# Two more token sets routed inside the attentions, and another order of dense chunks and quads in the last mixture

## The chip, the cores and the metric

The kernel runs on one core of one Trainium2 chip. The metric is the device time of one execution in microseconds. The engines are TensorE (PE, with its weight loads shown as PEld), VectorE (DVE), ScalarE (ACT), GpSimd (POOL) and SyncE (SP). Each engine works through its own instructions; transfers run on 16 DMA engines and are started by SyncE, ScalarE or GpSimd.

## The reference

The reference is a two-layer decoder over 32 sequences of 128 tokens, so 4096 tokens of 128 features. Each layer adds a self attention, a cross attention to a context and a mixture of experts. The change concerns the second layer: the end of its attentions, and its mixture.

```python
def _L1_ffn_ref(hidden_states, gate_w, expert_bias, w1, w2, w3, sw1, sw2, sw3):
    E, TOP_K = 16, 4
    router_logits = x @ gate_w.T
    biased = router_logits + expert_bias
    _, sel = lax.top_k(biased, TOP_K)
    raw = jnp.take_along_axis(router_logits, sel, axis=-1)
    rw = jax.nn.softmax(raw.astype(jnp.float32), axis=-1)
    g = jnp.zeros((T, E), x.dtype).at[jnp.arange(T)[:, None], sel].add(rw)
    for e in range(E):
        routed = routed + g[:, e:e + 1] * _swiglu(x, w1[e], w2[e], w3[e])
    shared = _swiglu(x, sw1, sw2, sw3)
    return shared + routed
...
x = x + _L1_attn_ref(_layernorm(x, axis=-1), ...)
x = x + _L1_xattn_ref(_layernorm(x, axis=-1), ctx_1024, ctx_1024, ...)
x = x + _L1_ffn_ref(_layernorm(x, axis=-1), ...)
```

## The kernel before

**Tokens.** The 4096 tokens are eight groups of 512 (`NG`), each of four batches of 128. Two groups make a set, so there are four sets, 0 to 3, of eight batches (`NBR`). In the second mixture set 1 (groups 2 and 3, the dense pair) is computed densely: every one of its tokens goes through all 16 experts, weighted with a share that is zero for the experts not chosen. Sets 0, 2 and 3 (`SETS`) are computed by rows: a token's row is written to the place of each of its four experts, the experts run over these rows alone, and the results are read back and added.

**The second layer's attentions** (`second_layers`) are written as a list of stages. A tuple (stage, at, every, n) says that the stage's k-th piece is issued in step at + every * k. `steps` goes through the steps and issues the pieces; stages in `between` are split into small parts, and one part is put after each part of the main stages, so that VectorE's and GpSimd's small work lies between the larger pieces. From step 8 on the order within each engine is that in which the code is written. Self attention runs ahead, cross attention (`xweights`, `xaverage`, `xfinish`) follows; it takes four batches per group, one batch per step, and ends in step 45. Before each product of a batch GpSimd copies v (line 1075). Inside these steps set 0 is already prepared for the mixture: `rnorm`, `rscaled` and `rturn` of groups 0 and 1 (steps 18 to 24), `routing` (step 25), the choice in parts (`choose`), `placed` (step 33, which counts and gives each token its places) and `way_out` (from step 35: GpSimd issues 32 indirect DMAs, line 2096, four per step, each of 128 rows of 512 bytes). The normed rows of a group are kept in `xn`, the transposed ones in `hs`.

**The last mixture** (`last_layer`) is a second such list, wholly in written order, SyncE's DMAs included. Its pieces are these.

- A *quad* is four tiles of 128 rows, each of one expert; there are 12 per set, 36 in all. `rows_of` loads 256 KB of rows and four blocks of 192 KB of weights, with room for three quads at once. `rows_turned` transposes the rows (line 2176), `rows_up` makes the gate and up products and the activation (lines 2188 and 2189), `rows_down` the down product one step later, and it stores 256 KB of results.
- A *chunk* is one expert over 512 tokens. `chunk_up` issues pg and pu on TensorE, the activation on ScalarE (line 2226), the product with pu on VectorE (line 2227) and, for an expert, the product with the share (line 2229). `chunk_down` issues y. The dense pair has 2 * 17 chunks, where the 17th is the shared expert. The groups of the row sets have just the shared expert, so six more chunks, called `alone`. After its last chunk a group's x is added by TensorE, copied and stored.
- `at` says which chunks are issued in which step. `ups` and `downs` go by it. With two chunks in a step, `downs` holds chunks back, so that the y of one comes after the pg and pu of later ones; with fewer than two it issues everything that waits, in that step:

```python
        def downs(s):
            while waiting and (len(at.get(s, ())) < 2 or not at.get(s + 1)):
                chunk_down(*waiting.pop(0))
                yield
```

- `fetched` loads the shares of four experts for a group, 1 MB, broadcast from DRAM, where `send` has put them.
- `way_back` issues four gathers of GpSimd (line 2204) for a batch, and `added` adds their rows to x on VectorE (line 2215). Three batches' gathered rows have room.
- `norm`, `scaled`, `turn`, `routing`, `chosen`, `placed`, `owned` and `way_out` prepare set 1 (up to `send`) and sets 2 and 3.

Before, the first quads begin with step 0, the dense pair is prepared in steps 0 to 4, set 2 in steps 1 to 10 and set 3 in steps 5 to 20. Chunks begin in step 6, with one beside each quad up to step 23 and one beside every second quad from then on; nine dense chunks and the six alone follow from step 38 on, two per step at first, with the gathers of set 3 one batch per step.

## Time and profile before

| | |
|---|---|
| time before, three runs | 1402.74, 1413.80 and 1420.57 us; median 1413.8 |
| the profiled execution's own time | 1410.02 us |
| its span in the profile | 1408.2 us |
| mean granted TensorE clock | 0.947 |
| busy: TensorE, VectorE, ScalarE, GpSimd | 1259.3, 858.3, 577.2, 534.6 us |
| moved by DMA | 129.06 MB, 92 GB/s in the mean |
| last projection of the cross attention starts | 1119.74 us |
| first and last transposes or products of the quads | 1121.3 and 1352.1 us |
| rows scattered by GpSimd in the last 300 us (line 2096) | 64 and 12 DMAs, 0.98 us each |
| rows gathered by GpSimd (line 2204) | 96 DMAs, 0.97 us each |

Times in views of the profile are in microseconds from the span's start. A line of a timeline names start, duration, engine, source line and operation, then output<-inputs by the program's names, the shapes and how many instructions are put together; what stands in brackets is the idle time ahead of them and what ended it. PE's records of one product come in pairs, so x2 is one product of 512 columns. The line of many matrix products is that of a helper, 977, so they are told apart by the names of their tiles.

### The profile page before, as it was taken

What the parts mean: (1) busy time and instruction counts of PE and PEld (TensorE: products, weight loads), DVE (VectorE), ACT (ScalarE), POOL (GpSimd) and SP (SyncE); (2) the same over time, 40 slices, a digit from 0 to 9 for tenths busy, and PEclk for the clock granted to TensorE, in tenths of its full rate; (3) what the DMA queues carried; (4) which work ended last, traced back from release to release, by engine and by line L of the source; (5) the groups of instructions that cost most, each with busy time, mean ns of one, the idle gap of its engine ahead of it and who ended that gap; (6) DMA issues with size and microseconds to landing.
All of it is one profiled execution on the core that took longest, in us unless ns stands there. A gap on an engine that the chain in (4) does not pass through costs nothing.

```text
span 1408.2 us, 27520 instructions
## 1 busy us (share of the span) xinstructions
PE 1259.3 (89%) x10753; PEld 846.7 (60%) x10753; DVE 858.3 (61%) x2271; ACT 577.2 (41%) x848; POOL 534.6 (38%) x729
## 2 busy tenths in 40 slices
PE   3689999999999999699999988989986688799997
PEld 2357777777777787444444445656653376577753
DVE  5646767676777575385775536666674346534563
ACT  1354445454554433133232235555543434334432
POOL 5233243435341231032000214444427605575775
PEclk8789999999999999799999999989987869999999
DMA  9501111121111111455055020000001259599943
GB/s 351 177 1 32 32 31 33 32 50 34 41 31 32 32 32 37 92 112 122 14 107 122 0 97 1 3 1 2 2 1 31 84 156 334 193 337 306 326 147 96
DMA packets 89528, 129.06 MB, mean 92 GB/s; under 512 B 9872, under 2 KB 63760, under 8 KB 87984
## 3 DMA queue, kind: packets, MB, share of 16 engines
q1 hardware_dynamic: 76624, 102.59, 26.0%
q0 software_dynamic: 6144, 12.60, 3.0%
q10 hardware_dynamic: 6624, 12.05, 2.3%
q8 instruction: 87, 1.43, 0.4%
q14 instruction: 49, 0.40, 0.1%
HBM read 99.34 MB, written 27.85 MB: 90 GB/s over the span
## 4 chain that ended last, share of the span: by engine, by line
PE 64%; DVE 15%; POOL 7%; DMA 5%; ACT 4%; issue 3%; SPq 1%; DVEq 0%; ACTq 0%; POOLq 0%
PE po L977 8%; PE pg L977 7%; PE pu L977 7%; PE y L977 6%; PE pqk L977 6%; PE scores L977 4%; PE sums L977 4%; PE xscores L977 3%; POOL rows_in L2096 3%; PE pval L977 3%; DMA factor<-factors 2%; PE pyrows L977 2%; PE proj L977 2%; PE xsums L977 2%; PE qkvr L977 2%
## 5 line engine op out<-in xcount | busy, mean ns | idle before, releaser
L1280 ACT ACTIVATE e<-scores 128x1024 f32<-128x1024 f32 x128 | 124.0, 1021 | 61.5 <-PE scores L977 61.5
L977 PE MATMUL y<-sg,wide 128*128 128x512 f32 x224 | 117.6, 613 | 7.5 <-DVE sg L2229 2.6
L977 PE MATMUL pg<-hx,wide 128*128 128x512 f32 x224 | 116.0, 599 | 0.0
L977 PE MATMUL pu<-hx,wide 128*128 128x512 f32 x224 | 115.3, 596 | 0.0
L2204 POOL DMA_INDIRECT back<-rows_out,place x96 | 93.1, 970 | 37.5 <-issue 24.6
L1295 DVE STREAM_TRANSPOSE by_token<-sums 128x512 f32<-128x512 f32 x64 | 45.6, 713 | 96.7 <-PE sums L977 96.5
L1126 POOL TENSOR_SCALAR xn<-x,mv,r 128x128 f32<-128x128 f32 x80 | 67.7, 853 | 91.7 <-PE pxn L1135 82.8
L1097 POOL TENSOR_SCALAR r<-mv 128x4 f32<-128x4 f32 x48 | 11.5, 241 | 219.4 <-DVE mv L1116 219.0
L1531 ACT ACTIVATE e<-xscores 128x1024 f32<-128x1024 f32 x64 | 62.0, 1021 | 79.9 <-PE xscores L977 79.9
L1882 ACT ACTIVATE sg<-pg 128x512 f32<-128x512 f32 x72 | 43.0, 597 | 119.4 <-PE pg L977 110.4
L977 PE MATMUL sums<-e,v 128*32 128x128 f32 x2048 | 74.8, 290 | 17.2 <-POOL v L1075 17.1
L977 PE MATMUL scores<-qb,k 32*128 32x512 f32 x512 | 79.1, 689 | 11.9 <-ACT qb L1466 4.5
L1883 DVE TENSOR_TENSOR sg<-sg,pu 128x512 f32<-128x512 f32 x72 | 49.3, 685 | 61.1 <-PE pu L977 58.1
L1097 POOL TENSOR_SCALAR r2x<-mv 128x2 f32<-128x2 f32 x16 | 3.7, 234 | 212.0 <-DVE mv L1116 212.0
L977 PEld LDWEIGHTS sums<-e,v 128*32 128x32 f32 x2048 | 55.7, 115 | 46.8 <-POOL v L1075 21.6
L2096 POOL DMA_INDIRECT rows_in<-xr,place x64 | 62.9, 983 | 34.6 <-issue 18.0
L1545 DVE COPY v<-pval 128x512 f32<-128x512 f32 x64 | 43.5, 680 | 51.1 <-PE pval L977 51.1
L1579 ACT COPY av<-po 128x512 f32<-128x512 f32 x64 | 37.5, 586 | 89.6 <-PE po L977 89.5
L977 PEld LDWEIGHTS pu<-hx,wide 128*128 128x128 f32 x224 | 42.6, 191 | 52.5 <-issue 50.1
L977 PE MATMUL po<-e,v 128*64 128x128 f32 x1024 | 65.8, 281 | 8.2 <-DVE v L1545 8.2
L977 PE MATMUL po<-av,wide 128*128 128x256 f32 x256 | 64.1, 405 | 8.1 <-DVE av L1599 8.1
L977 PEld LDWEIGHTS y<-sg,wide 128*128 128x128 f32 x224 | 35.9, 189 | 58.0 <-DVE sg L1885 36.7
(300 smaller groups left out, 2913.2 us busy)
## 6 DMA issues: line engine op xcount, KB each, us to landing
row_weights<-in_w1f_dram SPq DMA_DIRECT2D x144, 192.0 KB, 4.2
factor<-factors SPq DMA_DIRECT2D x64, 256.0 KB, 5.0
share<-combined SPq DMA_DIRECT2D x32, 512.0 KB, 11.4
rows_in<-in_few SPq DMA_DIRECT2D x36, 256.0 KB, 4.1
rows<-rows_in SPq DMA_DIRECT2D x36, 256.0 KB, 5.3
rows_out<-yrows ACTq DMA_DIRECT2D x36, 256.0 KB, 4.3
share<-combined SPq DMA_DIRECT2D x8, 1024.0 KB, 7.8
wide<-in_w1f_dram SPq DMA_DIRECT2D x1, 3272.0 KB, 10.5
```

The lines of the kernel that those rows point to most:

```text
L977: last[0] = nc.tensor.matmul(*args, **kw)
L1097: nc.gpsimd.tensor_scalar(t, src, add, None, ALU.add)
L1126: eng.tensor_scalar(n[:, b, :], x[g][:, b, :], mv[:, b, 0:1], r[:, b : b + 1], ALU.subtract, ALU.mult)
L1280: nc.scalar.activation(e[-1], ps[:, bass.ts(n, 2)].rearrange("p c i s -> p (c i) s"), AF.Exp, scale=scale)
L1295: nc.vector.transpose(tt.rearrange("p i t r -> p (i t r)"), po.rearrange("p i s -> p (i s)"))
L1531: nc.scalar.activation(e[-1], ps[:, n].rearrange("p r c s -> p (r c) s"), AF.Exp, scale=scale)
L1545: nc.vector.tensor_copy(v[:, bass.ts(n, XC), :], pv)
L1579: nc.scalar.copy(avs[w][n][:, :, bass.ts(b, S)], po)
L1882: nc.scalar.activation(sg, pg, AF.Silu)
L1883: nc.vector.tensor_tensor(sg, sg, pu, ALU.mult)
L2096: sent = nc.gpsimd.indirect_dma_start(out=rows_in[n], out_offset=bass.IndirectOffsetOnAxis(ap=self.places[n][:, k, u : u + 1], axis=0), in ...
L2204: nc.gpsimd.indirect_dma_start(out=outs[n, u][:, k], out_offset=None, in_=rows_out[n], in_offset=bass.IndirectOffsetOnAxis(ap=places[n][:, ...
```

## The change

The dense pair and set 2 are now normed, scaled, turned and routed inside `second_layers`, as set 0 was. Their turned rows go into the context's tiles that are not needed any more (`more`), and set 2's normed rows as well (`kept`). `choose(1, 3)` in steps 34 to 39 makes the dense pair's weights and `send` writes them to DRAM in step 41; set 2's logits come in step 41, and its choice is finished at the start of `last_layer`. Set 0's scatters are spread over steps 35 to 45, three per step.

In `last_layer` set 2's choice is in step 0, its places in step 1, its scatters in steps 2 to 5, eight per step; set 3 is prepared in steps 0 to 14. Dense chunks begin in step 0 (one, two and two in steps 0 to 2), the quads begin with step 3 (`Q` = 2). One chunk lies beside each quad in steps 3 to 8, one beside every third from step 9 on. The 13 dense chunks left and four of the shared-expert chunks follow from step 39 (`END`) on, one per step, the last two of these in steps 56 and 58. Set 3's gathers come in steps 40, 42 and so on to 54, and `added` three steps later.

```diff
         def turn(wk, g):
-            pool = edge if g in groups(0) else wk
-            hs[g] = pool.tile([128, GT], F32, name="hx", bufs=2 if g in groups(0) else 5)
+            pool, bufs = (edge, 2) if g in groups(0) else (wk, 5)
+            hs[g] = more[g] if g in more else pool.tile([128, GT], F32, name="hx", bufs=bufs)
             by_feature(xn.pop(g), hs[g])
...
         def kept(self, g):
-            self.xn[g] = self.spare[:, g]
-            return self.xn[g]
+            if g < 2:
+                self.xn[g] = self.spare[:, g]
+            elif g * GB // NBR in SETS:
+                self.xn[g] = cx[g - 2].rearrange("p (b f) -> p b f", f=D)
+            return self.xn.get(g)
...
-        for s in range(6, NQ + 1):
-            if s < 2 * QUADS or s % 2 == 0:
-                at[s] = [todo.pop(0)]
-        for s in range(NQ + 2, 100):
-            if not todo:
-                break
-            at[s] = [todo.pop(0) for _ in range(min(2, len(todo)))]
-        for k in range(0, 4, 2):
-            at[s + k // 2] = alone[k : k + 2]
-        at[s + 3], at[s + 5] = alone[4:5], alone[5:6]
-        LAST = s + 6
+        Q = 2
+        many = {0: 1, 1: 2, 2: 2, **{s: 1 for s in range(3, 9)}, **{s: 1 for s in range(9, NQ + Q + 1, 3)}}
+        for s, n in many.items():
+            at[s] = [todo.pop(0) for _ in range(n)]
+        END = NQ + Q + 1
+        for s, item in enumerate(todo + alone[0:4], END):
+            at[s] = [item]
+        at[s + 1], at[END + 19] = alone[4:5], alone[5:6]
+        LAST = END + 21
...
-                fetches.append(((g, j), 5 if before is None else step_of[before, NS * j + NS - 1] + 1))
+                fetches.append(((g, j), 0 if before is None else step_of[before, NS * j + NS - 1] + 1))
...
-            (each(rows_turned, quads), 1, 1, NQ),
-            (several(turn, of_set(dense_n)), 2, 1, 1),
-            once(routing, dense_n, 2),
-            (lambda _: send(wk, dense_n), 4, 1, 1),
-            (several(turn, of_set(n2)), 4, 1, 1),
-            once(routing, n2, 4),
-            once(tables.owned, n2, 8),
-            (several(turn, of_set(n3)), 10, 1, 1),
-            once(routing, n3, 10),
-            once(tables.owned, n3, 14),
+            (each(rows_turned, quads), Q + 1, 1, NQ),
+            (several(turn, of_set(n3)), 2, 1, 1),
+            once(routing, n3, 3),
+            once(tables.owned, n2, 3),
+            once(tables.owned, n3, 8),
             (ups, 0, 1, LAST),
-            (each(rows_down, quads), 2, 1, NQ),
-            (each(rows_up, quads), 1, 1, NQ),
+            (each(rows_down, quads), Q + 2, 1, NQ),
+            (each(rows_up, quads), Q + 1, 1, NQ),
             (downs, 0, 1, LAST),
...
-                once(several(norm, of_set(dense_n)), None, 0),
-                once(several(scaled, of_set(dense_n)), None, 1),
-                once(several(norm, of_set(n2)), None, 1),
-                once(several(scaled, of_set(n2)), None, 2),
-                once(chosen, dense_n, 3),
-                once(chosen, n2, 5),
-                once(several(norm, of_set(n3)), None, 5),
-                once(tables.placed, n2, 6),
-                *((each(tables.way_out, batches(n2)[i::2]), 7, 1, 4) for i in range(2)),
-                once(several(scaled, of_set(n3)), None, 8),
-                once(chosen, n3, 11),
-                once(tables.placed, n3, 12),
-                (each(tables.way_out, batches(n3)), 13, 1, NBR),
-                (each(way_back, batches(0)), 21, 1, NBR),
-                (each(added, batches(0)), 24, 1, NBR),
-                (each(way_back, batches(n2)), 29, 1, NBR),
-                (each(added, batches(n2)), 32, 1, NBR),
-                (each(way_back, batches(n3)), NQ + 3, 1, NBR),
-                (each(added, batches(n3)), NQ + 5, 1, NBR),
+                once(chosen, n2, 0),
+                once(several(norm, of_set(n3)), None, 0),
+                once(tables.placed, n2, 1),
+                (each(tables.way_out, to_send(n2, 2)), 2, 1, 4),
+                once(several(scaled, of_set(n3)), None, 1),
+                once(chosen, n3, 4),
+                once(tables.placed, n3, 5),
+                (each(tables.way_out, to_send(n3, 1)), 7, 1, NBR),
+                (each(way_back, batches(0)), 20, 1, NBR),
+                (each(added, batches(0)), 23, 1, NBR),
+                (each(way_back, batches(n2)), 28, 1, NBR),
+                (each(added, batches(n2)), 31, 1, NBR),
+                (each(way_back, batches(n3)), END + 1, 2, NBR),
+                (each(added, batches(n3)), END + 4, 2, NBR),
...
-            (first(rturn), 20, 4, R),
+            (first(rturn), 20, 4, 3 * R),
...
-            (first(routing), 25, 1, 1),
+            (first(routing), (25, 33, 41), 1, 3),
             (lambda _: tables.owned(0), 36, 1, 1),
+            (lambda _: send(early, 1), 41, 1, 1),
...
-                (first(rscaled), 19, 4, R, xturn),
-                (first(rnorm), 18, 4, R),
+                (first(rscaled), 19, 4, 3 * R, xturn),
+                (first(rnorm), 18, 4, 3 * R),
...
-                (lambda u: tables.way_out(0, u), 35, 1, NBR),
+                (lambda i: tables.way_out(0, to_send[3 * i : 3 * i + 3]), 35, 1, 11),
+                (lambda _: choose(1, 3), 34, 1, 6),
...
-        mixture1 = mixture("l1f", W1F, lambda lg, _: tables.route(lg, 0), 1, True, of_expert, tables.kept)
+        route = lambda lg, n: tables.route(lg, n) if n in SETS else route_softmax(lg, edge)
+        mixture1 = mixture("l1f", W1F, route, 1, True, of_expert, {2: cx[0], 3: cx[1], 4: cx[4], 5: cx[5]}, tables.kept)
```

## The prediction

> **What bounds the kernel now.** I read the page first (TensorE is busy 1259.3 of 1408.2 us), then the busy time in stretches, then the timelines of TensorE, VectorE and GpSimd where a stretch looked thin. Columns of the first view: bounds of the stretch, its length, busy us (and instructions) of PE, PEld, DVE, ACT and POOL, granted TensorE clock, DMA share, GB/s.
>
> ```profile
> 1080.00:1100.00 20.00, 9.35 (x85) 4.40 (x88) 5.39 (x17) 5.88 (x8) 15.84 (x21) 0.74 0.09 27
> 1120.00:1140.00 20.00, 17.15 (x89) 15.81 (x90) 9.97 (x41) 6.02 (x10) 2.92 (x6) 0.65 0.71 208
> 1140.00:1160.00 20.00, 15.65 (x88) 14.05 (x87) 5.37 (x27) 8.58 (x13) 0.00 (x0) 0.66 0.44 136
> 1200.00:1220.00 20.00, 13.74 (x87) 10.26 (x85) 9.17 (x34) 6.82 (x10) 13.93 (x14) 0.98 0.37 134
> 1240.00:1340.00 100.00, 98.23 (x630) 76.13 (x630) 47.23 (x94) 42.23 (x72) 69.56 (x73) 1.00 0.99 328
> 1360.00:1380.00 20.00, 20.00 (x54) 9.31 (x53) 12.78 (x27) 4.77 (x8) 15.43 (x16) 1.00 0.22 62
> ```
>
> The reader is to see five regimes. At 1080 to 1120 the attentions end with GpSimd full and TensorE idle. At 1120 to 1160 the mixture starts at a granted clock of 0.65 with DMA half used. At 1200 to 1220 both fall off. At 1240 to 1340 TensorE and DMA are full together, at 328 GB/s. After 1352 the dense chunks run TensorE full under the last gathers.
>
> How long one step is comes from TensorE's timeline (start, us, engine, line, output<-inputs, [idle before <-releaser]).
>
> ```profile
> 1295.10 0.60 PE L2176 MATMUL prows<-in_few,rows 128*128 128x128 f32 x4
> 1298.26 0.60 PE L2176 MATMUL prows<-in_few,rows 128*128 128x128 f32 x4
> 1298.70 1.02 PE L977 MATMUL pg<-hx,wide 128*128 128x512 f32 x2
> 1303.95 0.60 PE L2176 MATMUL prows<-in_few,rows 128*128 128x128 f32 x4
> ...
> 1368.32 1.02 PE L977 MATMUL pg<-hx,wide 128*128 128x512 f32 x2
> 1370.90 1.02 PE L977 MATMUL pg<-hx,wide 128*128 128x512 f32 x2
> ...
> 1389.95 1.02 PE L977 MATMUL pg<-hx,wide 128*128 128x512 f32 x2
> 1390.82 1.02 PE L977 MATMUL pu<-hx,wide 128*128 128x512 f32 x2
> 1392.69 1.12 PE L977 MATMUL y<-sg,wide 128*128 128x512 f32 x2 [0.85 <-DVE sg L2227]
> 1394.54 1.02 PE L977 MATMUL pg<-hx,wide 128*128 128x512 f32 x2
> ```
>
> A quad without a chunk takes 3.16 us (1295.10 to 1298.26), one with a chunk 5.69. Two chunks per step flow at 2.58 us each (1368.32 to 1370.90), since `downs` lags. A lone chunk per step (the one at 1389.95 is shared-expert work) is different: its `y` stands directly behind its own `pu`, so TensorE stops 0.85 us for VectorE's product, and with its eight additions of x it takes 4.59 us. VectorE's timeline shows what a dense chunk adds to that wait:
>
> ```profile
> 1365.16 0.69 DVE L2227 TENSOR_TENSOR sg<-sg,pu 128x512 f32<-128x512 f32 x1 [1.16 <-PE pu L977]
> 1365.88 0.69 DVE L2229 TENSOR_TENSOR sg<-sg,share 128x512 f32<-128x512 f32 x1
> ```
>
> A second product, by the share, 0.72 us later. For the attentions I took every fourth sum of the cross attention, which repeats every four steps:
>
> ```profile
> 873.75 0.72 DVE L1295 STREAM_TRANSPOSE by_token<-sums 128x512 f32<-128x512 f32 x1 [1.57 <-PE sums L977]
> 905.97 0.72 DVE L1295 STREAM_TRANSPOSE by_token<-sums 128x512 f32<-128x512 f32 x1 [1.42 <-PE sums L977]
> 942.39 0.72 DVE L1295 STREAM_TRANSPOSE by_token<-sums 128x512 f32<-128x512 f32 x1 [1.43 <-PE sums L977]
> 977.50 0.72 DVE L1295 STREAM_TRANSPOSE by_token<-sums 128x512 f32<-128x512 f32 x1 [1.42 <-PE sums L977]
> 1009.61 0.72 DVE L1295 STREAM_TRANSPOSE by_token<-sums 128x512 f32<-128x512 f32 x1 [1.43 <-PE sums L977]
> ```
>
> Cycles of 32.2, 36.4, 35.1 and 32.1 us. The second and third hold the norm, scaling and turn of groups 0 and 1; the fourth holds the routing of set 0.
>
> **The change, stage by stage.** I take three stages of the profiled execution: up to the last projection of the attentions (1119.5), from there to the end of the last `pyrows` (1352.1), and from there to the end (56.1 us to 1408.2). The run itself took 1410.0, and the median shown is 1413.8.
>
> *Attentions: +8.* Four groups more are normed, scaled and turned there. Each costs what groups 0 and 1 cost, (36.4 + 35.1)/2 - 32.2 = 3.5, so 14. Two more routings are 16 logits records each, 1.85 us at full clock (981.21), so 3.6. The softmax of the dense pair is VectorE work of the kind that made the fourth cycle no longer than the first: nothing while VectorE keeps its slack (about 15 busy of 20 us at most there), 4 us without it. `send` puts eight transposes on TensorE, about 1. Together 18.6. Against that, GpSimd issues its scatters in order with the copies of v that `sums` waits for, one per 1.27 us (1113.83, 1115.10, with v at 1116.06, and TensorE waits 3.07 us for it). Scatters go out three per step over steps 35 to 45 in place of four over 35 to 42, so about eight of 32 now stand behind the last v copy: 8 x 1.27 = 10.2 off. Bounds: +18.6 if none of that is given back, -3 if the work of groups 4 and 5 fits into the waits of 1080 to 1120 (16.4 us of TensorE waiting on GpSimd and VectorE). I take 18.6 - 10.2 = +8.
>
> *Start to last quad: 232.6 becomes 213, so -20.* What leaves it: four groups' turns and two routings, at half clock 1.8 and 3.4 us each pair (1127.64, 1129.43), and the stop at 1214 to 1221, where set 2's scatters were late for its first quad. They now start about 28 us after the stage begins and end near 70, and set 2's quads come near 100. What comes in, with 0 at the last projection: the first share is fetched into memory that the attentions free, 1 MB behind that projection, landing near 7 (its median from issue is 7.8, alone less). The first dense chunk multiplies at 8, and VectorE then works in written order through set 2's choice (4.2 plus a trip to ScalarE, 14), set 3's moments (1166.3 to 1169.6 in the trace, 3.3; 17), chunks 1 and 2 (1.4 each), the places (5.3) and the scaling (2.3): 28. Only then can TensorE turn groups 6 and 7, and chunks 3 and 4 follow: 34. Step 3, with the logits, a chunk and the first quad, ends at 43. Bounds for the step's start are 16 (everything but set 3's moments, scaling and five chunks is done before 0) and 40 (share late by 6 more).
>
> Steps 4 to 14 hold seven chunks: 5 x 5.69, then two of 5.69 and four of 3.5, and 4 for set 3's places and owners: 58, so 101. Steps 15 to 38 have one chunk in three: TensorE needs (5.69 + 3.16 + 3.5)/3 = 4.12 per quad. DMA needs 0.79 MB of weights, 0.26 read and 0.26 written per quad, and GpSimd's scatters and gathers bring 0.065 MB every 1.25 us beside them, 52 GB/s: 1.31/(0.328 - 0.052) = 4.7 us. The old kernel ran one chunk per two quads there at 4.45, with DMA at 0.96 to 1.00. I take 4.5, nearer to that measured row: 24 x 4.5 = 108, and with 4 for the last share and late loads 101 + 108 + 4 = 213. So fewer chunks beside the quads buy little: DMA takes over as the bound. Ends: the early start and TensorE's 4.12 give 25 + 58 + 99 + 4 = 186; the late start and 4.9 give 49 + 58 + 118 + 4 = 229.
>
> The Trainium skill, DMA: Bandwidth & Descriptors, section Bandwidth, puts the fabric's ceiling at 435 GB/s and a core's HBM limit at about 358. The row says 328 at share 0.99, and the row decides. By 358 a quad would need 4.3 us, as an estimate from that page, and the stage would be 5 us shorter; by 435 TensorE would bind at 4.12 and it would be 9 shorter.
>
> *After the last quad: 56 becomes 89, so +33.* 21 of 34 dense chunks go beside or ahead of the quads, so 13 and the six shared-expert chunks are left, one per step. `downs` flushes whenever a step has fewer than two. Each dense one therefore costs 2.74 (1389.95 to its `y`) + 0.72 for the second product + 0.89 = 4.35 in place of 2.58. The first is half covered by the last `pyrows` (1.7 after it): 1.7 + 12 x 4.35 + 0.9 for group 3's x + 6 x 4.59 = 82.3, and the last copy and store take 6.5 as now. The gathers, every second step, are not the bound any more: 32 x 1.25 = 40 plus 5 to start, and they wait for `added` of three before, at 8.7 us per batch. Bounds: +29 (a few records overlap) and +36 (an `added` of 1.5 us delays a product now and then).
>
> Sum: 8 - 20 + 33 = +21 on 1410.0, 1431. As a ratio that is 1.0146, and on the median of 1413.8 it gives 1434.
>
> **The rivals**, with times on the median as above.
>
> *The attentions pay in full* (slower). Place: steps 26 to 45. Price: +18.6, since groups 4 and 5 put about 2.9 us each of GpSimd work into the stretch where GpSimd is already full, which eats the relief. For it: 15.84 busy of 20 at 1080. Against: the last v copy then has fewer scatters ahead. Sum 18.6 - 20 + 33 = +32, so 1446. It decides once the attentions grow by over 15, which carries the sum past 28.
>
> *The start is short* (not slower). Place: the first three steps. Set 2's choice and places and the share's fetch would run under the attentions' last steps; set 0's moments for the old mixture already ran there (GpSimd's r at 1089.48). Step 3 then starts at 16, and the stage is 18 shorter still, -38: 8 - 38 + 33 = +3, 1417; with the attentions at -3, 1406. Against: the first product waits for the share, and VectorE's written order holds the choice behind it. It decides if the first quad's `pg` starts under 22 us after the last projection.
>
> *The lone chunks don't stop TensorE*, so the change does what it says and the end is bound by the gathers: 60 in place of 89, sum -8, 1406. Against it stands the row at 1392.69, where the next chunk's `pg` did not move ahead of the waiting `y`.
>
> **How the numbers follow.** The forecast gets 0.50, the full attentions 0.28, the short start 0.13, the gather-bound end 0.09. What this kernel's measurement can tell from no change is about 2%, 28 us, so the line is 1442. The forecast's own spread puts 0.13 of its 0.50 beyond it; of the full attentions, whose 18.6 leaves out any wait on GpSimd that grows, 0.27 of 0.28. Slower by over 2%: 0.40. The two rivals on the other side leave 0.05 for faster by over 2%. Within 2%: 0.55. Range: 1408 (the short start and the gather-bound end are near it) to 1460 (the full attentions with a late start).
>
> **What would show it.** Right: in the last 80 us `y` waits 1.5 to 1.6 us for L2229's product at each of 12 chunks, at about 4.35 us per chunk; quads of sets 2 and 3 come every 4.4 to 4.7 us with DMA near 1.0; the stop before set 2 is gone; TensorE is thin for some 30 us after the attentions. Wrong: chunks at 2.6 us in the end, quads at 4.1, or the first quad within 20 us.

## The result, and the profile after

The changed kernel takes 1461.85 us in the median of four runs (1458.92 to 1467.0), the kernel before 1415.03 (four runs, 1402.74 to 1420.57). The ratio is 1.0347, with a 95% interval of 1.0271 to 1.0423: slower by over 2%, which the prediction had given a chance of 0.40, and 28 us above its forecast of 1434. 1461.85 lies just above the range's upper end of 1460.

The spans of the two profiled executions differ by 54.0 us (1462.2 and 1408.2). They are cut as in the prediction, with one cut more at the start and the second cut at the end of the last projection (1120.5 before, where the prediction had 1119.5):

| us | before | after | difference | forecast |
|---|---|---|---|---|
| to the first sum of the second cross attention | 873.8 | 882.5 | +8.8 | none |
| from there to the end of the last projection | 246.7 | 253.9 | +7.2 | +8 |
| from there to the end of the last `pyrows` | 231.7 | 237.4 | +5.7 | -20 |
| from there to the end | 56.0 | 88.3 | +32.3 | +33 |

The first row lies ahead of what was changed. Other runs of the changed kernel took 873 to 886 there, and a run of the old one 885 (below, with one register load), so the 8.8 us are spread; without them the two profiles differ by 45, as the medians do (47). Two terms came out near their forecasts; the third was 25 us off.

The first view of after is the busy time in stretches, with the columns of the prediction's first view: bounds, length, busy us (instructions) of PE, PEld, DVE, ACT and POOL, granted clock, DMA share, GB/s.

```profile
1080.00:1100.00 20.00, 15.08 (x200) 9.24 (x199) 14.24 (x50) 11.79 (x15) 11.83 (x19) 0.93 0.10 31
1140.00:1160.00 20.00, 10.00 (x35) 5.69 (x35) 17.10 (x63) 3.10 (x5) 6.91 (x9) 0.74 0.81 293
1180.00:1200.00 20.00, 17.20 (x89) 13.04 (x87) 12.18 (x43) 7.45 (x12) 13.96 (x15) 0.83 0.77 238
1250.00:1350.00 100.00, 85.55 (x590) 70.11 (x588) 38.64 (x84) 38.24 (x65) 53.68 (x56) 1.00 0.93 295
1400.00:1420.00 20.00, 12.64 (x27) 4.91 (x28) 10.34 (x22) 2.39 (x4) 7.74 (x8) 1.00 0.10 26
```

1080 to 1100 is no longer GpSimd's. The stage then starts with VectorE nearly full and TensorE half idle. Between 1250 and 1350 **neither TensorE nor DMA is full**: 85.55 us of 100, share 0.93. Before, it was 98.23 and 0.99 in such a stretch. The end runs TensorE at 63% at full clock.

TensorE's timeline at the start of the stage (the last projection ends at 1136.5) and in the end; columns start, us, engine, line, output<-inputs, [idle before <-releaser]:

```profile
1136.30 1.02 PE L977 MATMUL pg<-ctx,wide 128*128 128x512 f32 x2
...
1142.30 1.60 PE L977 MATMUL y<-sg,wide 128*128 128x512 f32 x2 [4.12 <-DVE eq L1765]
...
1158.25 2.36 PE L1135 MATMUL pxn<-in_few,xr 128*128 128x128 f32 x8 [7.70 <-DVE xr L1126]
...
1166.97 0.60 PE L2179 MATMUL prows<-in_few,rows 128*128 128x128 f32 x4
...
1175.30 0.60 PE L2179 MATMUL prows<-in_few,rows 128*128 128x128 f32 x4
...
1378.97 1.13 PE L977 MATMUL y<-sg,wide 128*128 128x512 f32 x2 [1.57 <-DVE sg L2232]
...
1383.39 1.13 PE L977 MATMUL y<-sg,wide 128*128 128x512 f32 x2 [1.57 <-DVE sg L2232]
```

The first quad's transposes come 30.5 us after the last projection, step 4 begins at +38.8, and TensorE stops for VectorE twice on the way. The first stop is not VectorE's own work, though the view names an instruction of set 2's choice (`eq`): the `y` needs the product with the share, and VectorE itself waited for the share to land.

```profile
1141.46 0.69 DVE L2232 TENSOR_TENSOR sg<-sg,share 128x512 f32<-128x512 f32 x1 [2.49 <-DMA share<-combined]
```

The second stop, 7.70 us, is for the scaling (`xr`), which stands behind the places in VectorE's order. In the end each dense chunk takes 4.42 us, 1.57 of them the wait for the product with the share.

SyncE's timeline in the late quads; x4 are the four weight loads of a quad and x1 its rows, the duration runs from the first issue's start to the last one's end:

```profile
1306.84 3.61 SPq L2171 DMA_DIRECT2D row_weights<-in_w1f_dram  x4
1310.51 0.56 SPq L2157 DMA_DIRECT2D rows<-rows_in  x1
1311.65 3.05 SPq L2171 DMA_DIRECT2D row_weights<-in_w1f_dram  x4
1314.74 0.42 SPq L2157 DMA_DIRECT2D rows<-rows_in  x1
1316.42 3.74 SPq L2171 DMA_DIRECT2D row_weights<-in_w1f_dram  x4
1320.21 0.48 SPq L2157 DMA_DIRECT2D rows<-rows_in  x1
1321.27 3.06 SPq L2171 DMA_DIRECT2D row_weights<-in_w1f_dram  x4
1324.38 0.45 SPq L2157 DMA_DIRECT2D rows<-rows_in  x1
```

In these lines SyncE goes from one group of issues to the next with hardly a pause. The four loads alone take 3.05 us when nothing stops them, and the next four start 4.8 to 4.9 us after the last four. Why they take so long is in the line of the register load, as the view of one source line gives it (minimum, median and maximum ns of one, first and last start):

```profile
L2162 SPq TENSOR_LOAD <-owner x144: 260/272/1034, 1147.9 to 1365.7; - x144
```

Ahead of every weight load SyncE fetches the tile's expert into a register, 272 ns, computes the address and then issues, 333 ns; with the steps between, that is 0.9 us from one load to the next ((3.05 - 0.33)/3).

### The profile page after: what moved, and what is told of

It is laid out like the page before. It is cut to its first block, busy times and chain, and to the rows that moved or that the text cites. A ratio compares the mean times of both kernels' runs of the same rounds, so it can differ in the third digit from the quotient of the medians.

```text
span 1462.2 us, 27531 instructions
## 1 busy us (share of the span) xinstructions
PE 1276.8 (87%) x10753; PEld 845.7 (58%) x10753; DVE 854.2 (58%) x2263; ACT 574.6 (39%) x846; POOL 539.7 (37%) x737
## 4 chain that ended last, share of the span: by engine, by line
PE 61%; DVE 18%; DMA 8%; ACT 4%; POOL 4%; issue 3%; SPq 1%; ACTq 0%; DVEq 0%; POOLq 0%
PE po L977 7%; PE pg L977 7%; PE pu L977 7%; PE y L977 7%; PE pqk L977 5%; PE scores L977 5%; PE sums L977 4%; DMA row_weights<-in_w1f_dram 3%; PE xscores L977 3%; PE pval L977 2%; DMA factor<-factors 2%; ACT e L1280 2%; PE proj L977 2%; PE qkvr L977 2%; PE xsums L977 1%
## 5 line engine op out<-in xcount | busy, mean ns | idle before, releaser
L977 PE MATMUL y<-sg,wide 128*128 128x512 f32 x224 | 120.7, 628 | 34.6 <-DVE sg L2232 21.1
L1126 POOL TENSOR_SCALAR xn<-x,mv,r 128x128 f32<-128x128 f32 x84 | 71.8, 861 | 91.4 <-PE pxn L1135 82.7
L1884 DVE TENSOR_TENSOR sg<-sg,pu 128x512 f32<-128x512 f32 x72 | 49.3, 684 | 66.5 <-PE pu L977 63.7
L1097 POOL TENSOR_SCALAR r<-mv 128x4 f32<-128x4 f32 x48 | 11.5, 240 | 194.2 <-DVE mv L1116 193.7
L977 PE MATMUL pg<-hx,wide 128*128 128x512 f32 x152 | 80.7, 614 | 0.0
L977 PE MATMUL pu<-hx,wide 128*128 128x512 f32 x152 | 79.7, 606 | 0.0
L2230 DVE TENSOR_TENSOR sg<-sg,pu 128x512 f32<-128x512 f32 x40 | 27.4, 686 | 82.8 <-PE pu L977 76.8
L2192 DVE TENSOR_TENSOR sgrows<-sgrows,pu 128x512 f32<-128x512 f32 x36 | 24.7, 687 | 87.1 <-PE pu L977 87.0
```

The costliest lines, as they stand in the source:

```text
L977: last[0] = nc.tensor.matmul(*args, **kw)
L1126: eng.tensor_scalar(n[:, b, :], x[g][:, b, :], mv[:, b, 0:1], r[:, b : b + 1], ALU.subtract, ALU.mult)
L1884: nc.vector.tensor_tensor(sg, sg, pu, ALU.mult)
L2192: nc.vector.tensor_tensor(sg, sg, pu, ALU.mult)
L2230: nc.vector.tensor_tensor(sg, sg, pu, ALU.mult)
```

## The experiments

Runs of one profile are compared by the stages above. For scale: the end of the last `pyrows`, counted from the first transposes of the thirteenth quad (steps 15 to 38), lay 127.8 us behind it in the changed kernel and 126.3 and 129.7 in two other runs with the same quads and loads (scatters four per step, and the end in pairs); two runs with one register load differ by 5.2 from each other. A difference of 5 us in one look at that stretch is no finding; 15 is.

**Two chunks per step in the end.** The edit puts the dense chunks left in pairs, as in the kernel before, and the gathers in every step.

```diff
-        for s, item in enumerate(todo + alone[0:4], END):
-            at[s] = [item]
+        for s in range(END, 100):
+            if not todo:
+                break
+            at[s] = [todo.pop(0) for _ in range(min(2, len(todo)))]
...
-                (each(way_back, batches(n3)), END + 1, 2, NBR),
+                (each(way_back, batches(n3)), END + 1, 1, NBR),
```

> The changed kernel, but after the last quad two chunks per step as before, and set 3's gathers one batch per step. Theory (a lone chunk's y waits for its own products, 1.57 us each): the waits of y for L2232 vanish, TensorE needs about 55 us for the 19 chunks, and the stage from the last pyrows to the end falls from 88 to 56-62 us, so about 28 us off the total (some 1434). Rival (the gathers, spaced over every second step, hold the end): pairing alone moves it by under 5 us once the gathers take as long. Nothing ahead of the last quad changes by more than 3 us.

Measured: 1431.32 us, ratio to before 1.0107 (1.0058 to 1.0157). The end took 59.6 us in place of 88.3. Dense chunks came every 2.58 us without a stop. So the lone chunk, whose `y` is flushed in its own step, costs what the prediction said, and the four dense chunks more than in the kernel before, whose end took 56.0, cost 3.6 us. The gathers did not hold this end: the last one was issued 17 us before it, and TensorE waited 1.7 us in all, for the last two shared-expert chunks.

```profile
1413.73 0.94 POOL L2207 DMA_INDIRECT back<-rows_out,place  x1 [0.30 <-issue]
```

```profile
PE y L977 <- DVE sg L2230: 1.7, 2, 0.8
```

**What paces the late quads: buffers, bytes or SyncE.** Three edits, one cause each:

```diff
-            xq = wk.tile([128, 4, D], F32, name="rows", bufs=3)
+            xq = wk.tile([128, 4, D], F32, name="rows", bufs=4)
-                w = wk.tile([128, 3, S], F32, name="row_weights", bufs=12)
+                w = wk.tile([128, 3, S], F32, name="row_weights", bufs=16)
```

> The changed kernel with room for four quads' rows and weights in place of three, each loaded one step earlier. Steps 15 to 38 took 127.9 us, 5.33 per quad, where TensorE needs 4.12. Theory L (a round trip: a buffer is freed, SyncE issues, 4 to 5 us to land, and three buffers don't span it): 4.3 to 4.6 per quad, 18 to 24 us off. Theory B (the DMA engines are full): 5.1 to 5.4, under 5 us off. Theory S (SyncE's own issuing, about 4.2 to 4.8 per quad, sets the pace): SyncE's waits for buffers, 30 of 128 us, turn into issuing, 4.6 to 4.9, 10 to 17 us off.

Measured: 1459.28 us, steps 15 to 38 in 125.5. A fourth quad of buffers gives 2 us there, which is no finding. The buffers are not what held these steps. Steps 4 to 14 took 64.8 us with it, where the changed kernel and the two runs with the same quads and loads took 70.6 to 73.1.

```diff
-                src = every[:, bass.ds(e, 1), :].rearrange("p e f -> p (e f)")
+                src = every[:, bass.ds(e, 1), 0 : 2 * S].rearrange("p e f -> p (e f)")
```

> The changed kernel with 128 KB of weights loaded per tile in place of 192; the down product uses the up block again, so the same buffers are held as long and the same number of DMAs is issued. What it leaves out: the down weights. Theory B (bytes): 1.05 MB per quad in place of 1.31, so 4.2 to 4.4 us per quad, some 22 us off in steps 15 to 38. Theory L: a landing is shorter by up to 1 us, 4.9 to 5.1, 6 to 10 us off. Theory S: unchanged, 5.2 to 5.4.

Measured: 1449.81 us, steps 15 to 38 in 122.6. From 1250 to 1350 DMA moved 259 GB/s at share 0.86. A third of the weight bytes less gave 5 us, hardly more than the spread, where the bytes as the bound would have given 22; so bytes were at most a small part.

```diff
-                e = nc.values_load(
-                    owners[n][0:1, t : t + 1],
-                    (mybir.EngineType.SP,),
-                    ...
+                e = t * E // NT
```

> The changed kernel with the expert of each tile fixed in the program, so that SyncE loads no register ahead of the weights (about 1 us per quad between the rows' issue and the weights'). What it changes: which expert a tile is computed with. Bytes, buffers and the number of DMAs stay. Theory S: 4.3 to 4.7 us per quad, 15 to 24 us off. Theory L: the round trip is up to 1 us shorter over two steps, 4.8 to 5.1, 6 to 12 us off. Theory B: 5.2 to 5.4.

Measured: 1436.46 us, steps 15 to 38 in 111.1, 4.63 us per quad. With the same bytes, SyncE's timeline now has pauses, and the stretches view shows a hundred us with DMA full (0.95 over steps 15 to 38):

```profile
1309.80 1.75 SPq L2165 DMA_DIRECT2D row_weights<-in_w1f_dram  x4
1311.61 0.42 SPq L2157 DMA_DIRECT2D rows<-rows_in  x1
1313.60 2.19 SPq L2165 DMA_DIRECT2D row_weights<-in_w1f_dram  x4
1315.84 0.44 SPq L2157 DMA_DIRECT2D rows<-rows_in  x1
1318.43 1.77 SPq L2165 DMA_DIRECT2D row_weights<-in_w1f_dram  x4
```

```profile
1240.00:1340.00 100.00, 92.01 (x674) 78.50 (x674) 44.93 (x99) 43.85 (x75) 61.05 (x64) 1.00 0.99 340
```

The four loads take as little as 1.75 us where they took 3.05, and DMA goes from 295 GB/s to 340. Of the 16.7 us, nothing is due to bytes. TensorE's waits for rows and weights (who <- released by, total us, times, longest), in steps 15 to 38 of the changed kernel and then of this run, all but vanish:

```profile
PE pg L977 <- DMA row_weights<-in_w1f_dram: 8.4, 11, 1.8
PE prows L2179 <- DMA rows<-rows_in: 3.2, 2, 2.9
```

```profile
PE prows L2173 <- DMA rows<-rows_in: 1.3, 1, 1.3
```

**More issues, same bytes.** The first attempt was a second register load per tile. Its result is never used, so only one load per tile is in the program; of the other, a semaphore step stayed.

> The changed kernel with the expert of each tile loaded into a register twice on SyncE, and nothing else. Theory S: each load costs SyncE about 0.35 us, so 1.3 to 1.5 us more per quad: 6.4 to 6.9 us per quad in steps 15 to 38 in place of 5.33, 26 to 36 us more there. Theory B (DMA engines full): SyncE has slack, 5.3 to 5.6. Theory L: half of it shows over two steps, 5.8 to 6.1.

Measured: 1466.82 us, steps 15 to 38 in 138.1, with 144 register loads on SyncE as before. The line of the first load shows what is left of it:

```profile
L2162 SPq EVENT_SEMAPHORE  x144: 17/17/17, 1135.2 to 1368.8; - x144
```

It takes the time from one weight load to the next from 0.90 to 0.96 us, so 0.25 us per quad and 6 us in steps 15 to 38; the stretch is 8 to 12 us longer than in the three runs without it. So this is a small dose of SyncE work, not the large one that the expectation priced. The second attempt splits the transfers:

```diff
-                nc.sync.dma_start(out=w.rearrange("p k f -> p (k f)"), in_=src)
+                wf = w.rearrange("p k f -> p (k f)")
+                nc.sync.dma_start(out=wf[:, 0 : 3 * S // 2], in_=src[:, 0 : 3 * S // 2])
+                nc.sync.dma_start(out=wf[:, 3 * S // 2 :], in_=src[:, 3 * S // 2 :])
```

> The changed kernel, with each weight tile fetched by two transfers of half its columns, so eight issues per quad on SyncE in place of four; bytes and register loads are the same. S: four issues more of 0.33 us each, 1.3 us per quad and 32 us in steps 15 to 38: about 155 to 162 in place of 126 to 130, DMA share no higher than before, and a run of 1485 to 1495. B: 126 to 133, with the same GB/s. A middle value with a DMA share near 1.0 would mean that halving the rows of a transfer costs the DMA engines themselves, and would not tell the two apart.

Measured: 1506.79 us, steps 15 to 38 in 172.1, 44 more. The stretches view, and TensorE's waits for rows and weights:

```profile
1250.00:1350.00 100.00, 73.99 (x422) 58.20 (x420) 23.70 (x49) 27.53 (x47) 37.29 (x39) 0.88 0.77 222
```

```profile
PE pg L977 <- DMA row_weights<-in_w1f_dram: 29.4, 31, 3.0
PE prows L2181 <- DMA rows<-rows_in: 8.8, 8, 5.1
```

DMA's share fell to 0.77, so the DMA engines were not what slowed it. 44 us are more than the 32 expected, since I had priced an issue at its own 333 ns. By SyncE's waits in this stretch (21.0 us in all) its own work went from 4.0 to 6.3 us per quad, 0.57 per added issue, its own 333 ns and the address and semaphore work around it.

**One register load for four tiles.** Same transfers, same values, one TENSOR_LOAD of four registers (308 ns).

```diff
+            _, es = nc.values_load_multi_w_load_instructions(
+                owners[n][0:1, 4 * q : 4 * q + 4],
...
-            for t in range(4 * q, 4 * q + 4):
+            for e in es:
```

> The changed kernel, with one register load on SyncE for the four experts of a quad in place of four loads; transfers, their sizes and their addresses are the same, and the values are still read at run time. Theory S (SyncE's own issuing paces the late quads): three of four loads of 0.27 us and the register work around each go, some 0.9 us per quad, so steps 15 to 38, first transposes to last pyrows, fall from 126 to 130 to 106 to 112 us, and the run to about 1440. Theory B (the bytes pace them, and the fixed experts gained by something else, an earlier issue or other addresses): 124 to 130, and a run of 1455 to 1462.

Measured: 1455.42 us, steps 15 to 38 in 121.0. This is between the two theories, and the next run, with the same quads, had 126.2; so one load gains something between 0 and 9 us (two runs against three of 126.3 to 129.7), and I had expected 16 to 22. The view of SyncE's waits (who <- released by, total us, times, longest), in the changed kernel's steps 15 to 38 and then in this one's, says where it went:

```profile
SPq L2171 <- DMA rows_out<-yrows: 14.8, 11, 3.0
SPq L2171 <- PE pg L977: 6.5, 25, 0.4
SPq L2171 <- PE pyrows L977: 4.5, 16, 0.4
```

```profile
SPq L2171 <- DMA rows_out<-yrows: 30.7, 15, 4.9
SPq L2171 <- PE pyrows L977: 5.5, 20, 0.4
SPq L2171 <- PE pg L977: 4.6, 16, 0.6
```

With its own work cut from 4.0 to 3.0 us per quad, SyncE waits more for `rows_out`, the store of a quad's results. No data pass from that store to a weight load. The wait comes from the program: in the trace the transfers of SyncE and ScalarE take eight semaphores in turn (100 and 102 to 108) as completion counters, and each waits for its own, so for the one eight before. GpSimd's have eight others (111 to 118). With fixed experts these waits were 5.9 and 2.5 us. Put in one table, over the whole of steps 15 to 38, with SyncE's own work as (stretch - its waits)/24, so that waits which the view does not name count as work:

| steps 15 to 38 | SyncE's own work per quad | time per quad | DMA share | TensorE waits for rows and weights |
|---|---|---|---|---|
| fixed experts | 1.8 | 4.63 | 0.95 | 1.3 |
| one register load, two runs | 3.0 and 3.1 | 5.04 and 5.26 | 0.92 and 0.89 | 8.8 and 11.4 |
| changed kernel | 4.0 | 5.33 | 0.90 | 11.6 |
| one semaphore step more per load | 4.3 | 5.76 | 0.82 | 17.4 |
| split transfers | 6.3 | 7.17 | 0.75 | 39.1 |

With the same bytes in every row, a quad takes longer the more SyncE has to do, and DMA is less busy.

**The quads first.** The changed kernel with the end in pairs, and with the quads starting in step 0, chunks from step 2 on and set 3's preparation two or three steps later.

```diff
-        Q = 2
-        many = {0: 1, 1: 2, 2: 2, **{s: 1 for s in range(3, 9)}, **{s: 1 for s in range(9, NQ + Q + 1, 3)}}
+        Q = 0
+        many = {s: 1 for s in range(2, NQ + Q + 1) if s % 3 != 0}
...
-            (several(turn, of_set(n3)), 2, 1, 1),
+            (several(turn, of_set(n3)), 5, 1, 1),
```

> The changed kernel with the first quad in step 1 in place of 3, no dense chunk ahead of it, one chunk beside two of every three quads from step 2 on, set 3's preparation some three steps later, and two chunks per step in the end. Theory S (SyncE's issuing paces the quads at 4.7 to 5.3 us whatever stands beside them, so what counts is that its loads never stop): from the last projection to the last pyrows 190 to 205 us in place of 237, the end 57 to 60, total 1385 to 1405, below the kernel before. Rival (VectorE's chain of choice, places and scaling sets the start, wherever the quads stand): TensorE stops for 15 to 20 us among the first quads, 212 to 220 us, total 1412 to 1420.

Measured: 1429.69 us, ratio 1.0102 (1.0019 to 1.0184), so no better than with the end alone put right. The first quad came at +10.7 in place of +30.5, but the last ended at +236.8, outside both theories. TensorE's two longest waits and SyncE's order ahead of the second of them:

```profile
1146.22 1.11 PE L2179 MATMUL prows<-in_few,rows 128*128 128x128 f32 x4 [5.01 <-DMA rows<-rows_in]
1174.61 1.08 PE L2179 MATMUL prows<-in_few,rows 128*128 128x128 f32 x4 [9.13 <-DMA rows<-rows_in]
```

```profile
1152.89 3.39 SPq L2171 DMA_DIRECT2D row_weights<-in_w1f_dram  x4
1156.33 8.38 SPq L2140 DMA_DIRECT2D share<-combined  x3
1164.81 0.38 SPq L2157 DMA_DIRECT2D rows<-rows_in  x1
```

Three shares stood ahead of the fourth quad's rows in SyncE's queue, and 6.6 of their 8.38 us SyncE waited for the landing of a quad's store. From the last projection to the last `pyrows` TensorE's waits for VectorE fell from 18.9 us in the changed kernel to 8.7, and those for DMA rose from 16.6 to 25.5. What the early start gave, the loads took back.

The same with a fourth quad of buffers:

> The run before it with room for four quads' rows and weights. Theory S: what a fourth buffer takes off is SyncE's waiting for buffers alone, 3 to 8 us off the quads. Rival L (the round trip through the buffers): 15 us or more.

Measured: 1426.21 us (ten runs), ratio 1.0090 (1.0047 to 1.0133). Not told apart from the last.

**Scatters of set 0, four per step again**, as before the change:

```diff
-(lambda i: tables.way_out(0, to_send[3 * i : 3 * i + 3]), 35, 1, 11)
+(lambda i: tables.way_out(0, to_send[4 * i : 4 * i + 4]), 35, 1, 8)
```

> The changed kernel with set 0's scatters four per step over steps 35 to 42 again. Theory (copies of v queue behind the scatters): from the first sums of the cross attention to the last projection 260 to 264 us in place of 253.9 (250.7 to 257.4 in the other runs with the same attentions), and the rows of the first quad are ready earlier behind the projection. Rival (the scatters weren't on the path): 250 to 257.

Measured: 1455.25 us. From the first sum to the last projection 252.3, where the runs with three per step had 249.7 to 257.6, so the 10 us that I took off don't show in the total. TensorE's waits in that stretch show a part of them. For the copies of v it waited, in the kernel before and then in this run:

```profile
PE sums L977 <- POOL v L1075: 6.5, 4, 3.1
```

```profile
PE sums L977 <- POOL v L1075: 5.8, 4, 3.1
```

In the changed kernel this wait is gone, and seven of the 32 scatters stand behind the last copy of v. So the relief is some 6 us; the granted clock, 0.93 in this run and 0.91 in the changed kernel, may hide it in the total.

**Putting right what was found.** The end in pairs and one register load:

> The changed kernel with two dense chunks per step after the last quad (as in the run with pairs, 1431) and one register load per quad. If the two causes add: 1431 - 17 = 1414, with the end at 60 and steps 15 to 38 at 106 to 112; same as the kernel before. If B: 1425 to 1431.

Measured: 1425.07 us (ten runs), ratio 1.0073 (1.0037 to 1.0109). The end is 59.9 us, steps 15 to 38 are 126.2. So the sum of the two parts wasn't reached: one load took 6 us off the run with pairs, not 17. (The stretches are those of the profiled execution, which took 1440.29.) The old kernel with one register load:

> The kernel before with one register load per quad. Its quads alternate with chunks, a pair of quads needs 8.85 us of TensorE, and SyncE's issues came at 4.8 per quad there, so S gives little: TensorE and DMA are both full from 1240 to 1340. Expected 1405 to 1413, 0 to 8 us less than before; under 1400 would mean that SyncE held the old kernel as well, over 1416 that the one load with four results waits for something new.

Measured: 1412.15 us (ten runs), ratio 0.9977 (0.9933 to 1.0022). In the old order TensorE is the bound, and SyncE's waits there are mostly for TensorE (`pyrows` 28.1, `pg` 11.5 us): no difference that can be measured.

**The wait for the stores.** Moving the quads' stores to GpSimd gives them counters of their own.

```diff
-            nc.scalar.dma_start(out=four_tiles(rows_out[n], q), in_=y)
+            nc.gpsimd.dma_start(out=four_tiles(rows_out[n], q), in_=y)
```

The first four of these six runs fell on a chip on which the kernel before itself took 1539.8 us, the last two on another with 1534.5, so they can be compared with one another and with it alone.

> The changed kernel with one register load per quad, and the store of each quad's results issued by GpSimd in place of ScalarE. The program gives the transfers of SyncE and ScalarE eight completion counters in turn, and each transfer waits until the one eight before it has landed; so a weight load stops for a store whose quad TensorE has just finished. GpSimd's transfers have counters of their own. Theory W (with the issue cost cut, the stops for the stores take its place: 30.7 us of SyncE's waits in the run with one load, 14.8 in the changed kernel): these waits go to about 0, steps 15 to 38 take 108 to 114 us, DMA share near 0.95. Rival D (DMA was the bound already in the run with one load): 119 to 124.

> The changed kernel, four register loads per quad, with only the stores moved to GpSimd. S: SyncE's own issues, 4.05 us per quad, stay, and with what it waits for buffers it comes to 5.0 to 5.3 per quad: 119 to 126 us for steps 15 to 38. W alone: 112 to 118. D: 126 to 130.

> The changed kernel with one register load per quad and four quads of buffers in place of three, stores on ScalarE as they are. W: buffers don't bring the stores' landing forward, the waits for stores stay above 15 us, steps 15 to 38 take 116 to 123 us. If it was the buffers that held the run with one load: 108 to 114.

> Two dense chunks per step after the last quad, one register load per quad, and the stores on GpSimd. If all three add: t0 to last quad 220, the end at 60, so 1406 to 1416 and the same as the kernel before. If D: 1420 to 1428, as with the pairs and one load.

> The changed kernel with four register loads per quad and only the quads' stores moved to GpSimd, once more, on another chip than the one on which the kernel before took 1540 us. S: SyncE's own issues of some 4 us per quad stay and buffers add to them, 119 to 126 us for steps 15 to 38 and a run of 1450 to 1458. If the wait for the stores' landing is the larger part: 112 to 118. If neither matters: 126 to 130.

> Two dense chunks per step after the last quad, one register load per quad, stores on GpSimd, once more, on another chip than the one on which the kernel before took 1540 us. If SyncE's two holds (its issues, and its wait for the stores) are what made the quads slow: steps 15 to 38 at 108 to 116 us, no waits of SyncE for rows_out, 1406 to 1416. If DMA binds: 120 to 126 and 1420 to 1428.

Measured, in us:

| | run | steps 15 to 38 |
|---|---|---|
| one load, stores on GpSimd | 1518.3 | 148.7 |
| four loads, stores on GpSimd, twice | 1522.7 and 1511.2 | 149.4 and 147.9 |
| one load, four quads of buffers, stores on ScalarE | 1554.9 | 153.0 |
| end in pairs, one load, stores on GpSimd, twice | 1502.7 and 1498.7 | 147.4 and 149.8 |

The last row's runs are medians of four; the executions profiled took 1495.9 and 1515.0. SyncE's waits for `rows_out` were gone wherever the stores had moved, and steps 15 to 38 took 147 to 150 us with one load as with four. There SyncE waited for TensorE's `pyrows` above all (23.6 to 44.1 us of the stretch), so it was not the bound. On these two chips, then, something else held the quads, and the runs don't tell whether the stores' wait held them on the others. TensorE waited there for VectorE's product and hardly at all for loads, and VectorE in turn for something that the profile doesn't name; in the changed kernel's first profile these two lines stand at 2.5 and 0. The lines are those of four loads with stores on GpSimd, second run:

```profile
PE pyrows L977 <- DVE sgrows L2192: 24.2, 9, 5.0
```

```profile
DVE sgrows L2192 <- remote: 39.1, 6, 7.3
```

The kernel with all three parts is faster than the kernel before on both, 0.9799 (0.9719 to 0.9878) and 0.9715 (0.9628 to 0.9801); whether by 2% is unclear. It was not run elsewhere, and without a profile of the kernel before on such a chip I can't say which part gives it.

## Why the prediction was wrong, step by step

**Attentions, +8: +7.2.** The total held by luck: both of its parts were too large, and the errors cancelled. TensorE's busy time in this stretch grew by 7.9 us (205.9 to 213.8) and its waits for normed tiles by 6.5 (16.2 to 22.7), together 14 for my 18.6, and its waits for copies of v fell by 6.5 for my 10.2. This is from one profile of each; over all runs the stretch grew by 3 to 14. The rival in which the attentions pay in full is out: it needed 15.

**The first steps, 43 us: 38.8.** The mechanism was as described: TensorE waits first for the share's landing (4.12 us), and then, while VectorE goes in written order through set 2's choice, set 3's moments, the places and the scaling, for the last of these (7.70). The pieces were a little shorter than I took them: the first product with the share came at +5.0 for my 8, and the scaling ended at +23.6 for my 28. The short start is out: the first quad's `pg` came at +34.4, not under 22.

**Steps 4 to 14, 58 us: 70.8.** Here 12.8 us were missed. TensorE is busy for 59.9 of the 70.8, at a clock of 0.95, and waits 10.8, of which the view names the largest:

```profile
PE y L977 <- DVE sg L2232: 3.1, 2, 2.6
PE prows L2179 <- DMA rows<-rows_in: 2.6, 1, 2.6
PE pg L977 <- DMA row_weights<-in_w1f_dram: 2.4, 2, 2.2
PE pg L977 <- ACT hrows L2181: 1.9, 1, 1.9
```

The step that failed is the sum of TensorE's work with nothing for waits but the 4 us for set 3's places and owners. Of the 10.8 us, 5.8 are waits for VectorE and ScalarE, where set 3's choice and places stand in VectorE's order between the chunks' products, and 5.0 are for rows and weights that came late. With fixed experts the stretch was 69.7, so SyncE's register loads are not what made it long. With a fourth quad of buffers it was 64.8, and no wait for a load was left, so the late loads there seem to want room; that is one run.

**Steps 15 to 38, 4.5 us per quad: 5.33.** This is the larger miss, 15.8 us with the 4 us that I had added for late loads counted in. The step that failed is "I take 4.5, nearer to that measured row". I weighed TensorE's 4.12 against DMA's 4.7 and left out the engine that issues the transfers. The trace of before had it: from 1297.27 to 1340.02 SyncE issued the rows of ten quads, one per 4.75 us. TensorE's transposes of the last twelve quads, from 1295.1 to 1345.2, came every 4.55 (my 4.45 is near the 4.43 of a single pair), and the time from a quad's rows' issue to its transposes fell from 9.3 to 5.2 us meanwhile. So TensorE lived on what had been loaded ahead; such a lead can be spent for 50 us, but not for 128. The runs show both ends: with SyncE relieved 4.63, and DMA nearly full; with SyncE loaded more 7.17, and DMA idle for a quarter. With SyncE relieved the stretch took 111.1 us, about the 112 of the forecast, so, as far as this one run shows, what the sum lacked was SyncE's term, and TensorE's and DMA's were sized well enough.

What isn't settled is the middle. One register load takes a quarter of SyncE's work away and gains 0 to 9 us of the 16.7 that fixed experts gain. Its waits for the stores' landing doubled at the same time, which would account for it, but the runs without those waits fell on the two chips where something else held the quads. Fixed experts also change how many tiles in a row read the same expert's block (in both kernels the experts ascend from tile to tile), and no run separates that; the two runs that add SyncE work leave the experts as they are.

On the rate itself the Trainium skill, DMA: Bandwidth & Descriptors, section Bandwidth, has a core's HBM limit at some 358 GB/s. The fullest stretch here moved 340 at share 0.99, so the measured value is 5% lower, and it is the one to plan with here. The same page, section "Issuing engines are not separate DMA queues", holds that the time a sequencer takes to start a DMA is usually small beside the DMA itself. For one weight load here that is 0.9 us beside 3.9 from issue to landing (median of 144). But the transfers overlap one another and the issues don't: per quad, 4.0 us of SyncE's own work stood beside the 4.63 that a quad took with SyncE relieved.

**The end, +33: +32.3.** 4.42 us per chunk where 4.35 was worked out, with the wait at L2232 in every one, and 88.3 us where 89 was forecast. The run in pairs shows it from the other side. Its end took the 60 us of the rival with the gather-bound end, but that is a coincidence: TensorE's products filled it, not the gathers.

Of the 25 us missing, then, 12.8 lie in steps 4 to 14 and 15.8 in steps 15 to 38, less the 4.2 that the first steps were early. (In the prediction's sum, 21 on 1410.0 is a ratio of 1.0149, not 1.0146, which is less than 1 us.)

## What to carry to other kernels

An engine that only issues transfers has a rate too: count its register loads, address work and issues per unit of work, and put that beside TensorE's and DMA's time before taking the larger of two. A stretch in which the consumer runs faster than the loads are issued lives on a lead; ask how long it lasts. And a schedule that flushes one short chain per step puts the whole chain on the path, so chunks should be left over in pairs, not one by one.

## What the runs showed of the hardware

- A register load of one value on SyncE takes 272 ns in the median and up to 1034, one of four values 308. From one weight load to the next SyncE took 0.9 us with the address from a register of its own load, and 0.47 with a fixed address ((1.75 - 0.33)/3).
- Splitting each of a quad's four transfers of 192 KB in two made the quad 1.8 us slower, with DMA less busy than before.
- DMA moved 340 GB/s at share 0.99 over 100 us when the issues kept ahead (fixed experts).
- Two chips ran the kernel before at 1535 and 1540 us, the others at 1412 to 1416. Of the changed kernels' runs there, the stretch up to the first sum was as long as elsewhere (875 to 884 us), while the cross attention (264 to 269 us for 250 to 258) and the mixture were longer; why is not known.
